# Two-layer graph attention on one Trainium2 core: in the last pass, a piece of layer 1 changes places with the weight sums

## The chip, the core and the metric

The kernel runs on one core of one Trainium2 chip. The core has five engines that work side by side: TensorE (PE in the profile; its weight loads are PEld), VectorE (DVE), ScalarE (ACT), GpSimd (POOL) and SyncE (SP), which here issues transfers only. The metric is the device time of one execution in microseconds (us), as the median of three runs.

## The reference

Two layers over a graph of 4096 nodes with 512 features and a dense 0/1 adjacency matrix of 4096 x 4096, all in float32. Cut to what is computed:

```python
# layer 0: 8 heads of 64, attention over all nodes
feats = einsum('nf,hfo->hno', X, W)
dense = s_self[:, :, None] + s_neigh[:, None, :]     # from feats
dense = where(dense > 0, dense, 0.2 * dense) * A     # non-neighbours become 0, not -inf
out = softmax(dense) @ feats + b
x = layernorm(x + relu(out))
# layer 1: attention inside 32 graphs of 128 nodes
a = where(mask, (x @ Wq.T + bq) @ (x @ Wk.T + bk).T * scale, 0)
scores = (a + adj + adj) * where(mask, 1, -1e6)
x = layernorm(x + (softmax(scores) * mask) @ (x @ Wv.T + bv))
```

## The kernel before

Layer 0 takes nearly all of the time. Because a score is the sum of one term for the row and one for the column, its exponential is a product. The kernel keeps the column terms per head and node, and forms a running matrix `q` by one VectorE instruction for each head and each tile of 128 nodes: `q` = max(row term, column term) times the transposed adjacency tile `at` (L1386). For a tile of 128 nodes and a chunk of 1024 rows, TensorE then makes three sums, all of them accumulated in PSUM over the 32 tiles of a chunk:

- the A f products (`accf`, L1406): features times `at`, for the whole width of the array, 16 matmul records for each four tiles;
- the products with `q` (`acc`, L1426): 64 records for each four tiles, each in a strip of 32 columns;
- the weight sums (`dens`, L1440): for each tile a few columns `e_b` times `mark`, the matrix of 0s and 1s that tells which of two terms was the greater. They stand in strips too, with 6 columns each, and are made for eight tiles at once: after every second group of four tiles, that is after the odd groups 1, 3, 5 and 7.

A `mark` comes from `q`: seven of eight are made by ScalarE (a sigmoid, L1395), the eighth by VectorE (L1391). `q` has 6 buffers (L532), `mark` 18 (L533).

The main loop (`main_pass`) runs four passes, each with two heads (`r` = 0 to 3), each over four chunks of 1024 rows (`c` = 0 to 3), each over 32 tiles (`j`). The first three passes take eight tiles a cycle (`wide=8`); the last takes four, so a chunk of it has eight cycles, called groups 0 to 7 here (`j0 // 4`).

Layer 1 needs the rows of layer 0, which are complete for a chunk once the last pass has been through it. It is cut into pieces, generators that are advanced one step at a time, and these steps stand among the work of the last pass. A table written out by hand says which step stands where: `PLANS` (L1294) has for each group two strings, the first for the place between the A f products and the products with `q` (`pieces(c, j0 // 4, 0)`), the second for the place after the latter (`pieces(c, j0 // 4, 1)`). A letter is one step: `a` and `b` are two blocks of 512 rows in layer 1, `E` the step that turns the sums of the chunk before into rows (L1237 to L1261), `R` the start of a block, `F` the normalisation of its rows on VectorE. The steps of a block are, in order: two transposing steps (L975), two steps of a product with `M_sb` (L995, 16 records each), one with the scores (L1022) and the exponentials (L1047), one with two values and a transposition (L1067, L1096), the output of two row tiles (L1081), two more values (L1067, 16 records), and the output of the last two (L1081, 4 records).

In chunks 1 and 2 the second strings of the odd groups are `Fb`, `a`, `b` and none; in chunk 3 group 7 has `a`. In chunk 1, block `b` doesn't exist at first, so that `b` does nothing in groups 0 to 2. In chunk 0 the last pass has no pieces in the second place.

The order of TensorE's instructions is the program's (L455, `manual_schedule` for PE alone). For the other engines a scheduler sets the order when the kernel is built, except for a few instructions that are pinned. PSUM for layer 1's steps comes from three banks in turn (`misc`, L542).

Of the kernel before, what the change touches and what calls it, by code (L numbers as in the profile page):

```python
# [404 lines left out]
def adjacency_streamed_path(  # L405
# [710 lines left out]
    def bring(r, c, j):  # L1116

        if r:
            at = ats[r, c, j] = ring("at", atp, 6).tile([P, C], F32R, name="at")
            nc.sync.dma_start(at.bitcast(F32), at_d[c, j])  # L1120
            return
        if j % 2:
            return
        if j % 4 == 0 and (c, j) not in a_bs:
            load_adjacency(c, j)
        pairs = a_bs[c, j - j % 4].rearrange("p t n -> p (t n)").bitcast(BF16)
        pairs = pairs.rearrange("p (t k n) -> p t k n", t=CT, k=2)[:, :, j % 4 // 2, :]
        pt = misc([P, CT, P], BF16)
        for t in range(CT):
            nc.tensor.transpose(pt[:, t, :], pairs[:, t, :], ident_b)  # L1130
        both = pt.rearrange("p t n -> p (t n)").bitcast(FP8).rearrange("p (n k) -> p n k", k=2)
        for k in range(2):
            at = ats[r, c, j + k] = ring("at", atp, 6).tile([P, C], F32R, name="at")
            nc.scalar.copy(at, both[:, :, k])  # L1134
            nc.gpsimd.dma_start(at_d[c, j + k], at.bitcast(F32))  # L1135
# [162 lines left out]
    def run_plan(todo, pinned=False):  # L1298
        for k in todo:
            if k == "F":  # L1300
                plan[k](pinned)
                continue
            gen = ends[0] if k == "E" else plan[k]
            if gen is not None:
                next(gen)
            if k == "E":
                ends.pop(0)
# [3 lines left out]
    def run_pieces(budget):  # L1311

        state["credit"] += budget
        while state["credit"] > 0.0 and (work or ends):
            queue = ends or work
            try:
                state["credit"] -= next(queue[0])
            except StopIteration:
                queue.pop(0)
        if not (work or ends):  # L1320
            state["credit"] = 0.0
# [3 lines left out]
    def main_pass(r, ae=None, wide=4):  # L1325

        for c in range(NCH):
# [10 lines left out]
            def pieces(c, group, place):  # L1338
                if r == PR - 1 and c:
                    run_plan(PLANS[c == NCH - 1][group][place])  # L1340
                elif place == (r == 0):
                    run_pieces(0.75 * wide)

            def sums_over_a(c, cycle):
                for j in cycle:

                    a_j = ats[r, c, j].bitcast(BF16).rearrange("p (n k) -> p n k", k=2)
                    for s in range(2):
                        lo = 32 * (2 * (j % 2) + s)
                        nc.tensor.matmul(  # L1350
                            ae[lo : lo + NE + 1, :],
                            e_p[:, j, : NE + 1],
                            a_j[:, ts(s, HB), 1],
                            start=(j < 2),
                            stop=(j >= NT - 2),
                        )
# [4 lines left out]
            for j0 in range(0, NT, wide):  # L1361
# [60 lines left out]
                for j in cycle:  # L1422
                    for s in range(2):
                        for o in range(0, FP, 32):
# [5 lines left out]
                                start=(j == 0),  # L1430
                                stop=(j == NT - 1),
                            )
                pieces(c, j0 // 4, 1)

                done_j = j0 + wide
                for j in range(done_j - 8, done_j) if done_j % 8 == 0 else ():
# [9 lines left out]
                            )  # L1446
                if r == 0 and (c, j0 + wide) != (NCH - 1, NT):
                    sums_over_a(c, cycle)
                for x_ in follow[first:]:
                    bring(*x_)  # L1450
                group_0 = (at_step - NT * NCH) // 4
# [16 lines left out]
    with tc.tile_pool(name="ps_ae", bufs=1, space=PSUM) as psx:  # L1468
        ae = psx.tile([P, HB], F32, name="ae")
        nc.vector.memset(ae, 0.0)  # L1470
        banks.append(psx)
        main_pass(0, ae, wide=8)
        banks.remove(psx)
    first_pass.close()
    banks.extend([ctx.enter_context(tc.tile_pool(name="ps_misc2", bufs=2, space=PSUM))] * 2)
    with tc.tile_pool(name="wl1", bufs=1, side="right") as wp:
        work.append(weights_of_layer_1(keep, wp))
        work.append(kind_of_graphs(wp))
        work.append(kind_of_scores(wp))
        main_pass(1, wide=8)  # L1480
        for gen in work:
            for _ in gen:
                pass
        work.clear()
    main_pass(2, wide=8)
    more.clear()
    wide_passes.close()
# [60 lines left out]
```

## Time and profile before

| | us |
|---|---|
| median of 3 runs | 2067.35 (2067.16 to 2067.58) |
| the profiled execution | 2069.35 |
| its span, from the first instruction to the last | 2067.6 |
| VectorE: `q` (L1386), 1024 instructions, 1278 ns each | 1242.4 busy |
| ScalarE: `mark` (L1395), 896 instructions, 1145 ns each | 994.3 busy |
| PE: `acc` (L1426), 8192 records, 593 ns each | 902.8 busy |
| PE: `accf` (L1406), 2048 records, 398 ns each | 494.4 busy |
| PE: `dens` (L1440), 2048 records, 379 ns each | 124.5 busy |

The profile is of one execution. Busy time of PE is modelled, as matmuls overlap: four of them in different strips run at the same time, so 64 records of `acc` at 593 ns follow from start to end in 7 us. For PE the distance from the start of one group of matmuls to the start of the next is what counts. The last pass runs from 1361 to 1949 us of the span; what follows, to 2067.6, is what is left of layer 1.

### The profile page before, as it was taken

How to read it: one execution, taken by the hardware profiler on the slowest of the kernel's cores; microseconds unless marked ns; L12 is line 12 of the kernel's file. 1: busy time of each engine (PE TensorE's matmuls, PEld its weight loads, DVE VectorE, ACT ScalarE, POOL GpSimd, SP SyncE). 2: the span in 40 equal slices, each digit the busy share in tenths (PEclk: the TensorE clock that was granted, in tenths of full speed). 3: DMA queues.
4: the chain of work that ended last, by engine and by line, in shares of the span. 5: the costliest groups of instructions: out<-in, count | busy, mean ns of one | idle time of the engine just before them, and what ended most of it. 6: DMA issues, size and time to landing. Idle time of an engine off the chain costs nothing.

```text
span 2067.6 us, 38274 instructions
## 1 busy us (share of the span) xinstructions
PE 2032.2 (98%) x15086; PEld 1047.3 (51%) x15086; DVE 1670.1 (81%) x2125; ACT 1540.2 (74%) x1869; POOL 222.0 (11%) x361
## 2 busy tenths in 40 slices
PE   8999999999999999999999999999999999999997
PEld 6885555544445444444445444444454444445453
DVE  5667888888799998798999999999975984886654
ACT  3338888888878899788899899998885666567420
POOL 1223222222100000000000000000200210210111
PEclk9999999999999999999999999999999999999998
DMA  6989999999899999888999899989974773774211
GB/s 198 302 272 245 273 291 263 297 257 299 257 344 336 365 344 349 263 312 292 326 311 341 288 364 330 329 285 367 321 240 141 245 254 128 229 275 160 80 49 43
DMA packets 207371, 551.31 MB, mean 267 GB/s; under 512 B 24780, under 2 KB 65740, under 8 KB 207180
## 3 DMA queue, kind: packets, MB, share of 16 engines
q1 hardware_dynamic: 136716, 418.45, 57.8%
q0 software_dynamic: 62272, 121.91, 23.1%
q10 hardware_dynamic: 8192, 8.39, 1.2%
q8 instruction: 121, 1.98, 0.4%
q14 instruction: 70, 0.57, 0.1%
HBM read 491.79 MB, written 107.22 MB: 290 GB/s over the span
## 4 chain that ended last, share of the span: by engine, by line
PE 84%; DMA 6%; DVE 4%; issue 3%; ACT 2%; POOL 1%; ACTq 0%; POOLq 0%; DVEq 0%
PE acc L1426 36%; PE accf L1406 21%; PE ps_m L1067 5%; PE ps_fe L722 5%; PE ps_m L995 5%; PE dens L1440 5%; DMA at_d<-at 3%; DVE q L1386 3%; DMA a_b<-in_adj_dram 2%; PE ps_m L1022 1%; PE ps_m L1081 1%; PE ps_m L1130 1%; DMA xt_f<-in_x_dram 1%; PE ps_m L975 1%; PE ps_m L924 1%
## 5 line engine op out<-in xcount | busy, mean ns | idle before, releaser
L1386 DVE SCALAR_TENSOR_TENSOR q<-p_row,d_all,at 128x1024 f32<-128x1024 f32 x1024 | 1242.4, 1278 | 163.9 <-PE acc L1426 126.5
L1395 ACT ACTIVATE mark<-q,nb_all 128x1024 fp8e4<-128x1024 f32 x896 | 994.3, 1145 | 167.7 <-DVE q L1386 152.6
L1426 PE MATMUL acc<-q,g_s 128*32 128x512 f32 x8192 | 902.8, 593 | 1.1 <-DVE q L1386 0.4
L1426 PEld LDWEIGHTS acc<-q,g_s 128*32 128x32 f32 x8192 | 264.7, 110 | 593.8 <-issue 532.2
L1406 PE MATMUL accf<-at,f_s 128*128 128x512 f32 x2048 | 494.4, 398 | 1.9 <-issue 1.8
L1406 PEld LDWEIGHTS accf<-at,f_s 128*128 128x128 f32 x2048 | 380.2, 189 | 110.7 <-issue 29.1
L1151 ACT ACTIVATE ck<-ck,neg_half_f 128x1024 f32<-128x1024 f32 x128 | 145.9, 1140 | 27.1 <-DMA ck<-in_adj_dram 27.1
L1152 ACT ACTIVATE ck<-ck,neg_quarter 128x1024 f32<-128x1024 f32 x128 | 146.3, 1143 | 1.8
L1440 PE MATMUL dens<-mark,e_b 128*6 128x512 fp8e4 x2048 | 124.5, 379 | 1.6 <-ACT mark L1395 1.6
L722 PE MATMUL ps_fe<-w_sb_f,xT_f 128*128 128x264 f32 (+1 forms) x512 | 121.2, 395 | 4.5 <-ACT xT_f L653 4.5
L1134 ACT CAST at<-ps_m 128x1024 fp32r<-128x1024 fp8e4 x128 | 120.1, 1025 | 5.9 <-ACT mark L1395 3.1
L1067 PE MATMUL ps_m<-wvT,x1T 128*128 128x512 f32 x256 | 114.2, 594 | 0.0
L995 PE MATMUL ps_m<-x1T,M_sb 128*128 128x512 f32 x256 | 113.0, 595 | 0.9 <-ACT x1T L976 0.9
L722 PEld LDWEIGHTS ps_fe<-w_sb_f,xT_f 128*128 128x128 f32 x512 | 100.8, 200 | 18.8 <-ACT xT_f L653 4.9
L1271 POOL DMA_DIRECT2D hs_d<-hst x12 | 10.7, 893 | 832.3 <-DVE hst L1261 814.0
L1391 DVE TENSOR_SCALAR mark<-q,d_all 128x1024 fp8e4<-128x1024 f32 x128 | 95.8, 749 | 4.8
L1440 PEld LDWEIGHTS <-e_b 128*6 128x6 bf16 x2048 | 52.8, 86 | 81.8 <-issue 38.7
L1135 POOL DMA_DIRECT2D at_d<-at x128 | 69.0, 539 | 175.4 <-ACT at L1134 110.0
L995 PEld LDWEIGHTS ps_m<-x1T,M_sb 128*128 128x128 f32 x256 | 48.1, 190 | 62.5 <-issue 60.3
L1067 PEld LDWEIGHTS ps_m<-wvT,x1T 128*128 128x128 f32 x256 | 47.7, 190 | 57.1 <-issue 55.9
L1002 ACT ACTIVATE zT<-ps_m,zb 128x512 f32<-128x512 f32 x32 | 21.8, 682 | 71.1 <-PE ps_m L995 71.1
L1075 DVE TENSOR_TENSOR v_t<-ps_m,bv_row 128x512 f32<-128x512 f32 x32 | 21.9, 685 | 61.5 <-PE ps_m L1067 61.5
(185 smaller groups left out, 1084.2 us busy)
## 6 DMA issues: line engine op xcount, KB each, us to landing
at<-at_d SPq DMA_DIRECT2D x384, 512.0 KB, 6.1
f_s<-f_d SPq DMA_DIRECT2D x128, 512.0 KB, 7.4
at_d<-at POOLq DMA_DIRECT2D x128, 512.0 KB, 14.9
ck<-in_adj_dram SPq DMA_DIRECT2D x128, 512.0 KB, 5.4
g_s<-g_d SPq DMA_DIRECT2D x128, 256.0 KB, 5.9
f_d<-fst POOLq DMA_DIRECT2D x16, 1024.0 KB, 7.2
a_b<-in_adj_dram POOLq DMA_DIRECT2D x32, 512.0 KB, 16.1
p_row<-pu_d SPq DMA_DIRECT2D x32, 512.0 KB, 7.5
```

The lines of the kernel that those rows point to most:

```text
L722: nc.tensor.matmul(pf[:, q, :, cols], tile_j(xTs[k][:, c].rearrange("p u n -> p (u n)"), u), w_sb[:, c, 4 * q : 4 * q + 4, cols], start=(c ...
L995: nc.tensor.matmul(pz, L1["M"][:, f, ts(c, P)], x1T[:, f, :], start=(f == 0), stop=(f == FC - 1),)
L1067: nc.tensor.matmul(pv, x1T[:, f, ts(u, P)], L1["wvT"][:, f, :], start=(f == 0), stop=(f == FC - 1),)
L1134: nc.scalar.copy(at, both[:, :, k])
L1151: tc.keep_in_program_order(nc.scalar.activation(ck, ck, AF.Square, bias=neg_half))
L1152: nc.scalar.activation(ck, ck, AF.Abs, bias=neg_quarter, accum_out=binp[:, k : k + 1])
L1386: nc.vector.scalar_tensor_tensor(q, p_row[h], d_j, ats[r, c, j].bitcast(F32), op0=OP.max, op1=OP.mult)
L1391: nc.vector.tensor_scalar(mark, q, d_j, None, op0=OP.is_gt, saturate=False)
L1395: nc.scalar.activation(mark, q, AF.Sigmoid, bias=nb_all[:, j, hh : hh + 1], scale=BIG, saturate=False,)
L1406: nc.tensor.matmul(accf[:, s, :], f_s[j // 4][:, j % 4, w, :], ats[r, c, j][:, ts(s, HB)], start=(j == 0 and w == 0), stop=(j == NT - 1 an ...
L1426: nc.tensor.matmul(acc[o : o + 32, s, :], g_s[j // 4][:, j % 4, h, o % FH : o % FH + 32], qs[j, h][:, ts(s, HB)], start=(j == 0), stop=(j ...
L1440: nc.tensor.matmul(dens[lo : lo + 6, :], e_b[:, j, 2 * r + h, :], marks[j, h][:, ts(s, HB)], start=(j == 0), stop=(j == NT - 1),)
```

## The change

In `main_pass`, the call of the second piece (`pieces(c, j0 // 4, 1)`) is kept where it was for the first pass only (`r == 0`). For the other passes it stands after the weight sums, that is behind the loop with `dens` and ahead of the second half of the next tiles' loads.

```diff
@@ -1430,7 +1430,8 @@
                                 start=(j == 0),
                                 stop=(j == NT - 1),
                             )
-                pieces(c, j0 // 4, 1)
+                if r == 0:
+                    pieces(c, j0 // 4, 1)
 
                 done_j = j0 + wide
                 for j in range(done_j - 8, done_j) if done_j % 8 == 0 else ():
@@ -1446,6 +1447,8 @@
                             )
                 if r == 0 and (c, j0 + wide) != (NCH - 1, NT):
                     sums_over_a(c, cycle)
+                if r:
+                    pieces(c, j0 // 4, 1)
                 for x_ in follow[first:]:
                     bring(*x_)
                 group_0 = (at_step - NT * NCH) // 4
```

`pieces` takes its second argument as the group and the third as the place. In the passes 1 and 2 it does something at place 0 alone, in the first pass at place 1 alone; in the last pass, chunks 1 to 3, at both.

## The prediction

> **What bounds the kernel now.** I read the page first, then the busy time by stretch of the last pass (1361 to 1949 us), then its waits, and last the order of time on TensorE, ScalarE and VectorE around each place that the diff touches. The page's part 1:
>
> ```profile
> PE 2032.2 (98%) x15086; PEld 1047.3 (51%) x15086; DVE 1670.1 (81%) x2125; ACT 1540.2 (74%) x1869; POOL 222.0 (11%) x361
> ```
>
> TensorE (PE) is busy nearly without a gap, and in the stretches between 1550 and 1950 us it reads 49.6 to 50.0 of every 50 us. So the time of this part is the sum of the distances from one group of matmuls to the next on PE. The end of a matmul is modelled; I use starts alone. An odd group of four tiles in the last pass, now (order of time, PE: start, duration, work):
>
> ```profile
> 1642.95 7.07 PE L1426 MATMUL acc<-q,g_s 128*32 128x512 f32 x64
> 1649.95 7.13 PE L1067 MATMUL ps_m<-wvT,x1T 128*128 128x512 f32 x16
> 1657.02 1.90 PE L1440 MATMUL dens<-mark,e_b 128*6 128x512 fp8e4 x32
> 1658.85 3.96 PE L1406 MATMUL accf<-at,f_s 128*128 128x512 f32 x16
> 1662.65 1.88 PE L1081 MATMUL ps_m<-v_t,pT_f 128*128 128x512 f32 x4
> ```
>
> The reader is to see the order products (acc), second piece (L1067), weight sums (dens), A f products (accf), and the distance from acc to the work after accf: 1662.65 - 1642.95 = 19.70 us. The chunk's end and the next chunk's start show the neighbours that the change makes:
>
> ```profile
> 1766.74 7.03 PE L1067 MATMUL ps_m<-wvT,x1T 128*128 128x512 f32 x16
> 1773.60 3.73 PE L1022 MATMUL ps_m<-x1T,zT 128*128 128x128 f32 x32
> 1777.17 1.88 PE L1081 MATMUL ps_m<-v_t,pT_f 128*128 128x512 f32 x4
> 1778.99 7.08 PE L1426 MATMUL acc<-q,g_s 128*32 128x512 f32 x64
> 1785.88 1.91 PE L1440 MATMUL dens<-mark,e_b 128*6 128x512 fp8e4 x32
> 1787.72 3.92 PE L1406 MATMUL accf<-at,f_s 128*128 128x512 f32 x16
> ...
> 1801.49 3.70 PE L1067 MATMUL ps_m<-wvT,x1T 128*128 128x512 f32 x8
> 1805.03 0.60 PE L1096 MATMUL ps_m<-ident_f,ns 128*128 128x128 f32 x4
> 1805.47 3.60 PE L1067 MATMUL ps_m<-wvT,x1T 128*128 128x512 f32 x8
> 1808.50 4.22 PE L1406 MATMUL accf<-at,f_s 128*128 128x512 f32 x16
> 1812.56 1.88 PE L1081 MATMUL ps_m<-v_t,pT_f 128*128 128x512 f32 x4
> ```
>
> Here acc and dens use 32 and 6 columns of the array ("strips"), all else 128 ("full"). Distances: 16 full matmuls between full ones 1773.60 - 1766.74 = 6.86; acc before full work 7.00 (1649.95 - 1642.95), before dens 6.89; dens 1.84. Eight full ones take 3.43 (half of 6.86), but 3.54 right after acc (1805.03 - 1801.49): 0.11 for the step from strips to full. Eight full ones and accf after them take 7.09 (1812.56 - 1805.47), so accf after full work is 7.09 - 3.43 = 3.66, while after dens it is 3.80 (1662.65 - 1658.85).
>
> Two more places, at which PE stands still:
>
> ```profile
> 1477.25 9.46 PE L1426 MATMUL acc<-q,g_s 128*32 128x512 f32 x62
> 1486.12 0.60 PE L1440 MATMUL dens<-mark,e_b 128*6 128x512 fp8e4 x4
> ...
> 1505.21 7.07 PE L1426 MATMUL acc<-q,g_s 128*32 128x512 f32 x64
> 1513.15 7.11 PE L995 MATMUL ps_m<-x1T,M_sb 128*128 128x512 f32 x16 [0.86 <-ACT x1T L976]
> ```
>
> In the first, acc takes 8.87 to dens instead of 6.89: q comes late from VectorE, 1.98 lost. In the second, the second piece waits for ScalarE's copy of x1T, and 7.94 stands where 7.00 would.
>
> **What the Trainium skill says.** "TensorEngine Tiling (Array Packing)", Key Properties: changing the tiling mode drains TensorE. No price is given; the trace agrees with about 0.1 us a step (0.11 from acc to full, 7.00 against 6.89 on leaving acc). "TensorE: Matmul & The Clock Gate", Part 3, what overlaps: matmuls start and end in program order, so a weight sum that waits holds everything behind it on PE. The rows above agree, but for two acc records that start among the first dens records, in other columns, at 1486. The same page's table gives ScalarE and VectorE first-in first-out queues; VectorE's 3.71 us of idleness before L1083 at 1663.71, with q work next in its queue, fits. "ScalarE: Activation LUTs", What ACT_TABLE_LOAD costs: 1283 ns and a drain besides; the trace has 1.28 for the load, and the next ACTIVATE 1.29 after its start, so I count no drain.
>
> **The change part by part.** No instruction is added or removed. In passes 1 and 2 the place in question calls nothing, pass 0 keeps it, and in the last pass's first chunk it calls nothing, so only chunks 1 to 3 of the last pass matter. In even groups no weight sums follow, so the two positions are the same. In chunk 1, group 1 the piece is "F", VectorE alone; in group 7 of chunks 1 and 2 it is empty. There remain nine places: chunk 1 groups 3 and 5, chunks 2 and 3 groups 1, 3 and 5 (16 full matmuls each), and chunk 3 group 7 (4 matmuls of L1081). What is passed is dens, which is PE work without DMA, so no queue of SP or POOL changes its program order.
>
> A plain place: before, 19.70. After: acc before dens 6.89, dens 1.84, the piece after strips and before full work 6.86 + 0.11 = 6.97, accf after full work 3.66; sum 19.36. Gain 0.34: two of four changes of mode go. The places at 1548.87, 1720.28, 1814.36 and 1891.71 have 19.70 too, those at 1677.01 and 1848.42 0.5 more, for a q that stays late. Seven places: 2.4.
>
> Chunk 1, group 3: before, 1525.78 - 1505.21 = 20.57. After, the piece starts 6.89 + 1.84 = 8.73 after acc, past the 7.94 at which x1T is there; the wait lies behind dens, 19.36, gain 1.2. If the copy came over 0.8 later, the rest would be seen again.
>
> Chunk 3, group 7: before, from acc to L1022 1955.98 - 1938.26 = 17.72. After: 6.89 + 1.84 + L1081 (1.71 between full work, 1593.62 to 1595.33, + 0.11) + 6.86 = 17.41; gain 0.3.
>
> What the order adds: dens follows acc at once, without the 7 us in which marks could come late. In every one of the nine groups the last mark ends at most 0.2 us after acc; the closest is chunk 3, group 5, whose acc ends at 1898.79:
>
> ```profile
> 1896.55 1.28 ACT L1395 ACT_TABLE_LOAD   x1
> 1897.84 1.15 ACT L1395 ACTIVATE mark<-q,nb_all 128x1024 fp8e4<-128x1024 f32 x1
> 1899.01 1.28 ACT L1047 ACT_TABLE_LOAD   x1
> ```
>
> This mark is ready at 1898.99. It is of the group's last tile, which only the last 4 of 32 dens matmuls read, 28 x 0.057 = 1.6 after dens starts at 1898.6: 1.2 to spare. Behind a late mark would wait the piece, accf, and all of PE. That wait is not in the trace at these nine places: bound 0 (marks as now) to 1.98 a place (the worst late q); I take 0, since dens already follows acc at once in group 7 of chunks 1 and 2 without loss.
>
> The piece itself starts 1.84 - 0.11 = 1.7 later. Its results: v_t is made at 1659.32 though its matmuls ended at 1657.0, and is needed from 1662.65; zT likewise has over 5 us until its bank is wanted. Group 7 frees x1b later, which starts the loads for L1167 later (1956.19), but VectorE then idles 2.89 until 1960.13. Each costs nothing while these gaps stand, at most 1.7 if they don't.
>
> The earlier dens frees marks: there are 18 buffers, 16 for one pair of groups, so the third mark of the next group waits for dens (four marks from 1657.97, whose q began at 1651.55). They can go some 7 us earlier. PE wants the q of that group from 1664.46 only, so I count nothing.
>
> Sum: 2.4 + 1.2 + 0.3 = 3.9. The profiled execution (2069.35, span 2067.6) becomes 2065.45; it stands 2.0 above the median of the runs, and the same difference on 2067.35 gives 2063.5.
>
> **The rivals.** What is not fixed by hand is the order on the other engines: only PE's is. With dens earlier and pieces later, the order of q, marks and layer 1's own work on VectorE and ScalarE may come out differently.
>
> Late stages also shrink. Stalls of PE that remain: 1.6 at the starts of chunks 2 and 3 each (8.60 against 7.00), twice 0.5 in group 3, 1.2 before 1996.48; 5.4 together. If marks that leave ScalarE earlier took half of it, 2.7 more: 2060.8. For: VectorE waits for q buffers that marks hold, 0.98 at 1893.73. Against: the stalls at chunk starts come from VectorE's own load.
>
> The gain is given back: VectorE, busy 45 of 50 us from 1650 to 1700, sets the pace, so in the five places of groups 1 and 3 what PE saves returns as a longer wait for q: 4 x 0.34 + 1.2 = 2.6 go back, a gain of 1.3 is left, 2066.0. Against: VectorE stands idle 3.71 waiting for PE right there.
>
> Slower: marks or q are queued behind layer 1's work, and now meet PE at dens or acc. Place: the odd groups of chunks 1 to 3; price 1.98 each, as at 1477.25. Two such places eat the gain; from five on (9.9 against 3.9 + 4.1) the kernel is slower by over 0.2%. Six would give 2067.35 - 3.9 + 11.9 = 2075.4. For: margins of 1.2 us, and table loads of 1.28 between marks in groups 5. Against: the marks' place in program order is unchanged.
>
> **How the numbers follow.** From no change a measurement of this kernel can tell about 0.2%, 4.1 us, so below 2063.2 is faster and above 2071.5 slower. Main case 0.50, 2062 to 2065, time 2063.5: it lies just inside, 0.22 of it beyond 2063.2 and 0.28 within. Late stages shrink 0.16, all faster. Given back 0.14, all within. Slower 0.20, of it 0.19 over 2071.5. Faster 0.38, same 0.43, slower 0.19. The range 2059.8 to 2070.5 leaves out some 0.04 below and 0.14 above.
>
> **What would show it.** Right: acc to dens 6.89 in all odd groups, dens 1.84, accf after the piece about 3.66, 19.36 in all; no wait of L995 for x1T in chunk 1. Wrong: dens or acc stretched by 1 us or more after a mark or q; an accf still 3.8 long after the piece; a stall in the part after 1949 that has grown.

## The result and the profile after

| | before | changed |
|---|---|---|
| median of 20 runs each, us | 2068.15 (2065.18 to 2071.67) | 2065.69 (2063.72 to 2068.84) |
| ratio changed to before | | 0.9987, 95% interval 0.9981 to 0.9992 |
| the profiled execution, us | 2069.35 | 2068.04 |
| its span, us | 2067.6 | 2066.2 |

The kernel became faster by 0.13%: 2.7 us by the ratio (the medians differ by 2.5), with an interval of 1.7 to 3.9. The forecast was 3.9 us (0.19%), just inside the 0.2% that was called no change. Two later comparisons, each with both kernels on one chip, gave 0.998 (0.997 to 0.999) and 0.9982 (0.9975 to 0.9988), that is 4.1 and 3.7 us.

The same group of the last pass as shown above, now in the changed kernel (order of time, PE: start, duration, work):

```profile
1642.85 7.07 PE L1426 MATMUL acc<-q,g_s 128*32 128x512 f32 x64
1649.74 1.91 PE L1441 MATMUL dens<-mark,e_b 128*6 128x512 fp8e4 x32
1651.58 7.13 PE L1067 MATMUL ps_m<-wvT,x1T 128*128 128x512 f32 x16
1658.15 4.23 PE L1406 MATMUL accf<-at,f_s 128*128 128x512 f32 x16
1662.22 1.88 PE L1081 MATMUL ps_m<-v_t,pT_f 128*128 128x512 f32 x4
```

The weight sums (dens) now follow acc 6.89 us after its start, the piece comes behind them, and the work after accf starts at 1662.22 - 1642.85 = 19.37 us, where it was 19.70. The group in which L995 waited for ScalarE's copy of x1T:

```profile
1506.61 7.08 PE L1426 MATMUL acc<-q,g_s 128*32 128x512 f32 x64
1513.50 1.91 PE L1441 MATMUL dens<-mark,e_b 128*6 128x512 fp8e4 x32
1515.34 7.13 PE L995 MATMUL ps_m<-x1T,M_sb 128*128 128x512 f32 x16
1521.91 4.23 PE L1406 MATMUL accf<-at,f_s 128*128 128x512 f32 x16
1525.98 4.45 PE L995 MATMUL ps_m<-x1T,M_sb 128*128 128x512 f32 x10
```

There is no wait at L995 any more, and the distance is 19.37 as well, where it was 20.57. (The x10 of the last line counts only what the view holds; the group has 16 records.) TensorE's waits in the last pass and its rest, first in the kernel before, then in the changed one (who waited for whom: us in total, times, longest):

```profile
PE ps_m L975 <- DVE x1b L520: 1.2, 1, 1.2
PE ps_m L995 <- ACT x1T L976: 0.9, 1, 0.9
PE acc L1426 <- DVE q L1386: 0.4, 2, 0.2
PE ps_m L1260 <- DVE nm_f L1031: 0.2, 1, 0.2
```

```profile
PE ps_m L975 <- DVE x1b L520: 1.9, 1, 1.9
PE acc L1426 <- DVE q L1386: 0.4, 2, 0.2
PE ps_m L1260 <- DVE nm_f L1031: 0.2, 1, 0.2
```

One wait is gone, and no wait of dens for a mark has come. But the first, in the tail of the kernel, is 0.7 longer. The sum over the part with all nine places makes the account. From the start of acc in chunk 1, group 2 to its start in chunk 3, group 7 it was 445.62 us and is 442.15; the last place (acc of group 7 to L1022) was 17.72 and is 17.42. Together 3.77 us. The spans differ by only 1.4, since in this one execution of the changed kernel chunk 0 of the last pass took 98.87 us instead of 97.08, and the tail's wait grew. Chunk 0's loss is seen on VectorE:

```profile
1444.17 0.56 DVE L1167 SCALAR_TENSOR_TENSOR x1b<-hp_l,x1b 128x384 f32<-128x384 f32 x1 [3.77 <-DMA hp_l<-hs_d]
```

VectorE stands 3.77 us at this instruction for a load (2.48 at the same one before), the q behind it come late, and acc (group 6) takes 8.52 instead of 7.15. Chunk 0 has the same instructions in the same order in both kernels, so this was taken for an accident of one execution; the experiments below bear on it.

### The profile page after: what moved, and what is told of

Same layout as the page of the kernel before. It is cut to its first block, busy times and chain, and to the rows that moved or that the text cites. A ratio compares the mean times of both kernels' runs of the same rounds, so it can differ in the third digit from the quotient of the medians.

```text
span 2066.2 us, 38253 instructions
## 1 busy us (share of the span) xinstructions
PE 2030.9 (98%) x15086; PEld 1049.8 (51%) x15086; DVE 1670.1 (81%) x2125; ACT 1540.4 (75%) x1869; POOL 222.9 (11%) x361
## 4 chain that ended last, share of the span: by engine, by line
PE 84%; DMA 7%; issue 4%; DVE 2%; ACT 1%; POOL 1%; POOLq 0%; ACTq 0%; DVEq 0%; SPq 0%
PE acc L1426 36%; PE accf L1406 20%; PE ps_m L1067 5%; PE ps_fe L722 5%; PE ps_m L995 5%; DMA at_d<-at 5%; PE dens L1441 5%; PE ps_m L1022 1%; DVE q L1386 1%; PE ps_m L1081 1%; DMA xt_f<-in_x_dram 1%; ACT mark L1395 1%; PE ps_m L975 1%; PE ps_m L1130 1%; PE ps_m L924 1%
## 5 line engine op out<-in xcount | busy, mean ns | idle before, releaser
L1151 ACT ACTIVATE ck<-ck,neg_half_f 128x1024 f32<-128x1024 f32 x128 | 146.0, 1141 | 21.7 <-DMA ck<-in_adj_dram 21.7
L1152 ACT ACTIVATE ck<-ck,neg_quarter 128x1024 f32<-128x1024 f32 x128 | 146.4, 1143 | 1.7
L995 PE MATMUL ps_m<-x1T,M_sb 128*128 128x512 f32 x256 | 112.9, 595 | 0.0
L995 PEld LDWEIGHTS ps_m<-x1T,M_sb 128*128 128x128 f32 x256 | 48.0, 190 | 59.3 <-issue 58.4
```

The lines of the kernel that those rows point to most:

```text
L995: nc.tensor.matmul(pz, L1["M"][:, f, ts(c, P)], x1T[:, f, :], start=(f == 0), stop=(f == FC - 1),)
L1151: tc.keep_in_program_order(nc.scalar.activation(ck, ck, AF.Square, bias=neg_half))
L1152: nc.scalar.activation(ck, ck, AF.Abs, bias=neg_quarter, accum_out=binp[:, k : k + 1])
```

## The experiments

The theory: the gain is what TensorE's own order costs, two changes between strips and full width less at each of nine places (0.34 us each), and one wait for x1T that is hidden behind the weight sums. The rivals: marks come free earlier, so that ScalarE and with it q come earlier; or the other engines got a better order, because the scheduler has other times to plan by. A further rival, that the gain comes from fewer changes of data type on TensorE, falls by counting: dens works on 8-bit marks and accf on another 32-bit format (`F32R`) than acc and the piece. In the order before, the type changes three times from acc to the work after accf, in the new order four times, and yet it is faster.

**One matmul of the piece ahead of the weight sums** (from the changed kernel). The piece is cut after its first matmul, at the eight places with 16 records:

```diff
                 if r == 0:
                     pieces(c, j0 // 4, 1)
+                elif r == PR - 1 and c and (c, j0 // 4) in SPLIT:
+                    next(plan[PLANS[c == NCH - 1][j0 // 4][1][-1]])
```

Here `SPLIT` holds the eight places, and the generators of L995 and of the second values yield once more, after their first matmul; the rest of the step runs at its place behind the weight sums.

> At the eight places with 16 matmuls the first matmul of the piece (two records, 0.43 us) stays between acc and the weight sums, and the other 14 records follow the weight sums. So the weight sums are early as in the changed kernel (0.5 us later than there, 6.5 us earlier than before), but the array changes between strips and full width four times again instead of twice. If the gain is that of the changes of mode: acc to the work after accf is back at 19.7 us at the plain places (19.37 in the changed kernel), in chunk 1 group 3 the wait for x1T is back too (20.6), and the kernel stands 2.7 to 3.9 us above the changed one, a ratio to before of 0.9995 to 1.000. If the gain is that marks are freed earlier, or that the weight sums are done earlier: 19.4 us, ratio 0.9985. If it is that the other engines got a better order: that order stays near the changed kernel's, so 19.4 too.

Measured: ratio to before 1.0003 (0.9994 to 1.0011), 4.6 us above the changed kernel on the same chip. The same group, in order of time on PE:

```profile
1642.11 7.07 PE L1436 MATMUL acc<-q,g_s 128*32 128x512 f32 x64
1649.12 1.13 PE L1069 MATMUL ps_m<-wvT,x1T 128*128 128x512 f32 x2
1650.17 1.90 PE L1453 MATMUL dens<-mark,e_b 128*6 128x512 fp8e4 x32
1652.00 6.28 PE L1069 MATMUL ps_m<-wvT,x1T 128*128 128x512 f32 x14
1657.71 4.23 PE L1416 MATMUL accf<-at,f_s 128*128 128x512 f32 x16
1661.78 1.88 PE L1085 MATMUL ps_m<-v_t,pT_f 128*128 128x512 f32 x4
```

1661.78 - 1642.11 = 19.67. The expectation had the size of the matmul wrong: 16 records take 6.86 us between full-width work, so two take 0.86, not 0.43. Here they take 1.05 from start to start (1649.12 to 1650.17), and acc ahead of them 7.01 instead of 6.89; these 0.3 us are the two changes of mode. In chunk 1, group 3 the wait is back, and with it 20.59 us:

```profile
1504.36 7.07 PE L1436 MATMUL acc<-q,g_s 128*32 128x512 f32 x64
1512.30 1.10 PE L995 MATMUL ps_m<-x1T,M_sb 128*128 128x512 f32 x2 [0.87 <-ACT x1T L976]
```

From chunk 1, group 2 to chunk 3, group 7 it is 445.52, as before the change (445.62), though the weight sums start 8.06 us after acc: 1.2 later than in the changed kernel (6.89), but 6.0 earlier than before (14.07). VectorE, ScalarE, GpSimd and SyncE run their instructions in exactly the changed kernel's order in the two traces. So neither the early weight sums nor the other engines' order is the gain.

**One place alone** (from the kernel before):

```diff
-                pieces(c, j0 // 4, 1)
+                moved = (r, c, j0) == (PR - 1, 1, 12)
+                if not moved:
+                    pieces(c, j0 // 4, 1)
 ...
+                if moved:
+                    pieces(c, j0 // 4, 1)
                 for x_ in follow[first:]:
```

> The kernel before, with the piece moved behind the weight sums in chunk 1 group 3 alone. If the wait of L995 for x1T lies behind the weight sums there: 19.4 us from acc to L995 of the next group instead of 20.57, no wait for x1T, and the seven plain places stay at 19.7 (20.2 where q is late), so 1.2 us less in the profile's sum and a ratio of 0.9994, which the timing can hardly tell from 1. If the wait only moves (ScalarE's copy comes later because marks take its place): 20.2 or more.

Measured: ratio 0.9993 (0.9984 to 1.0001). On PE:

```profile
1505.00 7.07 PE L1426 MATMUL acc<-q,g_s 128*32 128x512 f32 x64
1511.89 1.91 PE L1442 MATMUL dens<-mark,e_b 128*6 128x512 fp8e4 x32
1513.73 7.13 PE L995 MATMUL ps_m<-x1T,M_sb 128*128 128x512 f32 x16
1520.30 4.23 PE L1406 MATMUL accf<-at,f_s 128*128 128x512 f32 x16
1524.38 6.17 PE L995 MATMUL ps_m<-x1T,M_sb 128*128 128x512 f32 x14
```

The last group is cut by the end of the view again. 1524.38 - 1505.00 = 19.38, and the plain places stay at 19.70 (20.15 where q is late): the part with all places takes 444.38, 1.24 less than before. The time can't tell it from no change, the trace can. VectorE's and GpSimd's order is that of the kernel before. In the last pass ScalarE's and SyncE's differ only behind the copy of x1T, and that copy ends 7.80 us after acc starts, where it ended 7.79 after it before. So the copy comes no sooner; the wait for it is hidden behind the weight sums.

**The first pass too** (from the changed kernel). The call at the old position goes, the one behind the weight sums and the sums over A is made in every pass:

```diff
-                if r == 0:
-                    pieces(c, j0 // 4, 1)
 ...
-                if r:
-                    pieces(c, j0 // 4, 1)
+                pieces(c, j0 // 4, 1)
```

> The changed kernel with the piece behind the weight sums in the first pass too, that is behind dens and the sums over A, right ahead of the transposes of the next tiles (L1130). By the changes of mode alone: nine places in pass 0 with a piece, two changes each, 0.34 us: 3 us less than the changed kernel, ratio to before 0.997. The rival: the piece and L1130 share two PSUM banks, and the bank that L1203 fills comes free 4.3 us after L1203 starts (319.23 to 323.52 in the changed kernel, with 0.33 us of it as a wait); with 4 us less between them, L1130 waits 2.8 us longer at each of the three L1203 places, 8.5 us, and up to 1 us at the six others, so 5 to 11 us more than the changed kernel, ratio to before 1.001 to 1.004.

Measured: 2101.17 us, ratio 1.0151 (1.0136 to 1.0167). The rival came true, but at 35 us where 5 to 11 were put down. Pass 0 takes 459.5 us from its first acc to the next pass's, where the changed kernel takes 423.8. One of the three bad places, on PE:

```profile
320.38 0.66 PE L1203 MATMUL ps_m<-ident_f,hst 128*128 128x128 f32 x4
320.87 0.61 PE L1130 MATMUL ps_m<-ident_b,a_b 128*128 128x128 bf16 x8
325.63 1.03 PE L1130 MATMUL ps_m<-ident_b,a_b 128*128 128x128 bf16 x8 [4.15 <-DVE hst L1214]
326.42 9.81 PE L1406 MATMUL accf<-at,f_s 128*128 128x512 f32 x32
```

The second half of the transposes waits 4.15 us (0.33 in the changed kernel) until VectorE has read the bank that L1203 filled. That was foreseen. What wasn't: the places with L1237 and L1260 wait too, 2.2 and 2.6 us, where at most 1 was allowed for; and after most of these waits TensorE itself is slow. The accf shown takes 9.81 instead of 7.57, as its records follow each other at 0.43 us up to 331.25 and at 0.23 after that. The slow ones read tiles of `at` that ScalarE had made by 307.3, so it isn't `at` that is late. The trace shows the clock granted to TensorE at half from 324.4 to 331.2 us, and in eight stretches of pass 0, 30.6 us together; in the changed kernel's pass 0 it is full throughout. In chunk 1 the three places lose 6.2, 2.1 and 4.3 us (acc to acc 33.19, 28.63 and 31.23 instead of 27.00, 26.50 and 26.96), in the two chunks after it 3.8 to 5.0 each. So the place of a piece in the first pass is set by the two banks, which the piece and the transposes of the next tiles use in turn, and the 0.34 of the modes is small against that.

**The last block's rows in their own buffers** (from the changed kernel). Only the last block has its x and its earlier heads' rows in buffers of q, which are free by then (`RowsInQ`, a small class that isn't shown, makes two of them look like four rows):

```diff
-        x1b = lp.tile([P, 4, F], F32, name="x1b")
+        last = blk == NT // 4 - 1
+        if last:
+            own = [qp.tile([P, C], F32, name="q") for _ in range(4)]
+            x1b = RowsInQ(own[:2], F)
+        else:
+            x1b = lp.tile([P, 4, F], F32, name="x1b")
 ...
+            if last:
+                hp = own[2 + u // 2][:, ts(u % 2, C // 2)][:, : F - FP]
+            else:
+                hp = lp.tile([P, F - FP], F32, name="hp_l")
```

> The changed kernel, with the rows of the last block of layer 1 (x and the earlier heads' rows, 8 loads) in buffers of q, which nothing uses after the last pass, instead of in the two buffers that the block before still holds. If the idle time of TensorE before the last block's transposes (1.3 us in the kernel before, 2.0 in the changed one, from L891 to L975) comes from those loads, which can only start when the buffers come free: it goes to 0.2 or less, and the kernel is 1.2 to 2.0 us faster than the changed one, ratio to before 0.9970 to 0.9985. If VectorE's own work on these rows sets it (stats, L1167, L1009): no change in the gap, ratio 0.998 to 0.999.

Measured: 2065.06 us, ratio 0.9977 (0.9968 to 0.9987), where the changed kernel on the same chip had 0.9982. In the tail, first of the changed kernel and then of this one, on PE:

```profile
1992.74 0.19 PE L891 MATMUL dens<-ones_col,okp 128*1 128x1 f32 x2
1994.83 1.99 PE L975 MATMUL ps_m<-ident_f,x1b 128*128 128x128 f32 x16 [1.90 <-DVE x1b L520]
```

```profile
1992.50 0.19 PE L901 MATMUL dens<-ones_col,okp 128*1 128x1 f32 x2
1992.63 1.99 PE L985 MATMUL ps_m<-ident_f,q 128*128 128x128 f32 x16
```

The wait is gone: the loads are issued from 1939.11 on instead of 1980.42. Of the 2 us, 0.54 are given back earlier, where TensorE now waits 0.69 us at L1278 for VectorE, which stands 3.62 us for a load of the block before. It is the best version of this study, by point estimate: against the changed kernel, 1 us in the medians is too little to be shown by these times, as the intervals overlap.

**Rows in program order** (from the changed kernel):

```diff
-                nc.vector.scalar_tensor_tensor(dst, src, 0.0, dst, op0=OP.max, op1=OP.add)
+                tc.keep_in_program_order(
+                    nc.vector.scalar_tensor_tensor(dst, src, 0.0, dst, op0=OP.max, op1=OP.add)
+                )
```

> The changed kernel, with the adding of the earlier heads' rows (L1167) kept in program order on VectorE, where the scheduler had put some of them far ahead, in chunk 0, in front of q. If the stalls of chunk 0 that differ from run to run (acc to acc 12.6 to 14.3 in group 3, 10.9 to 12.4 in group 6) come from VectorE standing at L1167 for a load: these distances are 12.6 and 10.9, and chunk 0 takes 97.0 us rather than 97.1 to 98.9. In return the work stands at the start of chunks 1 to 3, where VectorE is short of time: up to four times 0.5 us more in each, so 0 to 6 us slower in all, ratio to before 0.998 to 1.002. If the stalls have another cause: chunk 0 stays at 97 to 99 from run to run.

Measured: 2072.35 us, ratio 1.0014 (1.0007 to 1.0021). Chunk 0 takes 96.38 us, less than in any other profile, with 12.58 and 10.85 in groups 3 and 6. So those stalls are VectorE's stands at L1167. The other profiles agree: in chunk 0 VectorE waits there for loads for 3.7 us in all before the change, where chunk 0 is shortest, and for 5.8 to 5.9 in the three profiles in which it is longest. But the work now stands at the chunks' starts; chunk 1, group 1 on PE:

```profile
1471.65 3.92 PE L1408 MATMUL accf<-at,f_s 128*128 128x512 f32 x16
1477.29 3.11 PE L1428 MATMUL acc<-q,g_s 128*32 128x512 f32 x18 [1.71 <-DVE q L1388]
```

The acc that starts so late has 64 records, of which the view holds 18. That chunk's first cycle takes 13.12 instead of 11.30, and the part with the nine places 447.01 instead of 442.15. It costs more than chunk 0 gives back, and a little more in all than was put down for it: 6.3 us against the changed kernel on the same chip.

**The changed kernel again, twice:**

> The changed kernel again, on the same chip as the others, to compare them with: ratio to before 0.9987 as measured (0.998 to 0.9995). The nine places as in its first profile: 19.37 us. The chunk 0 stall of 1.4 us (acc 8.51 at 1440.50), if it was an accident of one transfer: gone, or elsewhere. If it belongs to the change: there again.

> The changed kernel on the same chip as the two others, for comparison: ratio to before 0.9982 (0.997 to 0.9992), the nine places at 19.37, 19.86 where q is late, and 1.9 to 2.1 from L891 to L975 in the tail.

Measured: ratios 0.998 and 0.9982. The distances of all profiles, worked out from the starts of groups on PE (us):

| profile | chunk 0 of the last pass | chunk 1 group 2 to chunk 3 group 7 | L891 (its second record) to L975 in the tail |
|---|---|---|---|
| before | 97.08 | 445.62 | 1.34 |
| changed | 98.87 | 442.15 | 2.06 |
| changed, again | 98.84 | 442.18 | 1.93 |
| changed, third | 97.82 | 442.18 | 2.21 |
| one matmul ahead | 97.96 | 445.52 | 1.04 |
| one place | 97.55 | 444.38 | 1.95 |
| the first pass too | 98.74 | 442.19 | 2.08 |
| own buffers in the tail | 98.55 | 442.18 | 0.10 |
| rows in order | 96.38 | 447.01 | 1.77 |

The middle column repeats to 0.04 us in five profiles with the changed order; the two other columns vary by 1 to 2 us with the loads. In chunk 0 the loss isn't at one place either: group 6 in the first profile of the changed kernel (12.41 us from acc to acc instead of 10.85), group 3 in the second (14.33 instead of 12.58). Whether the change has a part in chunk 0 isn't shown: there are two profiles of the old order (97.08 and 97.55), and all with the changed order and the rows as they were lie above them.

For the tail the traces say more. VectorE stands there at L1167 for the load of one row tile, first before the change, then after it:

```profile
1989.68 0.56 DVE L1167 SCALAR_TENSOR_TENSOR x1b<-hp_l,x1b 128x384 f32<-128x384 f32 x1 [0.70 <-DMA hp_l<-hs_d]
```

```profile
1988.04 0.56 DVE L1167 SCALAR_TENSOR_TENSOR x1b<-hp_l,x1b 128x384 f32<-128x384 f32 x1 [1.42 <-DMA hp_l<-hs_d]
```

From issue to landing this load takes 3.31 us before and 4.03 in the changed kernel. But it takes 3.91 in the kernel with one place moved, whose tail is that of before, and 3.00 in the one with a matmul ahead, whose tail is that of the changed kernel. So the 0.7 us follow the load, and no run shows that the change makes it longer.

## Why the prediction was right

- The neighbours. Each number of the sum was read where the new neighbours already stood side by side: acc to dens 6.89 and dens 1.84 were forecast, 6.89 and 1.84 came, in all nine places but the two with a late q, where dens begins among the last matmuls of acc as at 1486 before. The piece with accf was put at 6.97 + 3.66 = 10.63 and takes 6.57 + 4.07 = 10.64; only the border between the two was wrong. The lines read for it had that border already (1805.47 to 1808.50 is 3.03 for the piece, not 3.43, and accf 4.06). A plain place was to be 19.36 and is 19.37 or 19.38.
- Chunk 1, group 3: forecast 19.36 and a gain of 1.2; 19.37 and 1.20. The copy of x1T was ready in time (7.80 us after acc's start, where the piece starts 8.73 after it).
- Chunk 3, group 7: forecast 17.41, measured 17.42.
- The sum: 3.9 forecast, 3.77 in the trace. Seven places at 0.31 to 0.34 make 2.3, not 2.4.
- The danger, dens right behind acc: forecast no wait. At the closest place, chunk 3, group 5, acc starts at 1889.97 and the last mark is this one, on ScalarE:

```profile
1896.10 1.15 ACT L1395 ACTIVATE mark<-q,nb_all 128x1024 fp8e4<-128x1024 f32 x1
```

It ends at 1897.25, 0.39 after dens began at 1896.86, and the last four matmuls, which read it, come 1.6 after that begin. The margin of 1.2 was there, and ScalarE's other work didn't move into it.
- The rivals. Late stages didn't shrink: both chunk starts keep 8.60 and 8.61, group 3 of chunks 2 and 3 keeps its 0.5 for a late q (19.86 against 19.37). The gain wasn't given back by VectorE, though it is busy for nine tenths there. The slower case didn't come.
- A step that was off without harm: marks were to go some 7 us earlier. They go 1.45 earlier (four marks from 1656.52 instead of 1657.97). On ScalarE they stood behind two steps of the check that the adjacency holds 0 and 1 alone (L1151, L1152), and now stand behind one, which waits for a load; and the third q, which the first of them reads, is made only by about 1655. Nothing was counted for it.
- One of the signs of being wrong came: the stall after 1949 grew (1.2 to 1.9 us). It doesn't speak against the sum, as the load behind it varies as much among kernels with the same tail. Another, an accf still 3.8 us long behind the piece, came by its letter (4.07), but the piece ahead of it is shorter by as much.
- The measured 2.7 us lies below the 3.77 of the trace's places, which are inside its interval of 1.7 to 3.9; the two later comparisons gave 4.1 and 3.7. A stall that differs from one execution to the next by up to 1.8 us in chunk 0 is enough for such a spread. So it is the trace, place by place, that shows the sum; that a total comes near to it is in part luck. The median of 2065.69 itself lies just above the main case's 2062 to 2065, with a kernel before that took 0.8 us more than the one the forecast started from.

## What to carry to other kernels

When TensorE has no gaps, the order of its groups is a cost in itself: put groups that use the array in the same way side by side, and read the price from a place in the same trace where the new neighbours already meet. A wait that other work can fill is worth more than the order (0.86 against 0.33 here), but look first at who shares the buffers that the moved work fills: in the first pass the same move costs 35 us. And where a gain of a few us is to be shown, distances inside one trace tell more than the total, if the total carries waits for loads that differ by as much.

## What the runs showed that was not expected

- A change between strips of the array and its full width costs 0.15 to 0.17 us on TensorE here (0.33 us for two fewer, 19.70 to 19.37; 0.30 for two more, 19.37 to 19.67). A small piece between two groups in strips pays it twice: two records of 0.86 us took 1.05, and acc in front of them 0.1 more.
- When accf follows full-width work, its first record starts 0.4 us before that work's share of time is over (6.57 instead of 6.97), and accf takes as much longer (4.07 instead of 3.66). The start of a group alone would have shown a gain that isn't there.
- In the first pass waits of 2.2 to 4.2 us on TensorE cost more than their own length: in most cases its clock fell to half behind them for 3.4 to 6.8 us.
- VectorE's stands for loads of row tiles, hoisted ahead of q by the scheduler, make the last pass's chunk 0 vary between 97.1 and 98.9 us. In program order it took 96.4 in the one profile taken, but the kernel is then 6.3 us slower.
